# One PSUM bank with four kinds of users: features one stage later, transposes at other stages

## Chip, cores and metric

The kernel runs on one core of a Trainium2 chip. The metric is the device time of one execution in microseconds (us), as the median of several runs.

## What is computed

Input x has 32 images of 256 channels and 32 x 32 pixels. Two layers follow each other, each added to its own input:

```python
# layer 0: group norm, then a 3x3 convolution as a product of values rounded to 16-bit floats
x = x + conv3x3(quantize(group_norm(x)), quantize(weight)) + bias
# layer 1: group norm, then an involution: a 7x7 kernel for each pixel, made from the pixel's features
n = group_norm(x)                                # 32 groups of 8 channels
y = relu(batch_norm(w1 @ n))                     # 256 -> 64 features
w = w2 @ y + b2                                  # 16 groups x 49 taps for each pixel
x = x + sum over the 49 taps of w[group, tap, pixel] * shifted n[channel, pixel]
```

## The kernel before

**Work of an image.** The function `front` is a generator that does everything of an image up to its features: sums of both channel halves, means, squares, variances (class `GroupNorm`), the convolution in four units of 18 matmuls (two channel halves x 9 taps), the second group norm, the normalized image `xn`, then the features and the transposes. It gives way with `yield`, and what stands between two yields is a *stage*. The features are 64 matmuls into `py` (line 366), which ACT turns into `y_sb` (line 373). The transposes are four times: 16 matmul instructions on TensorE (PE) into `pt` (line 381) and one copy by ScalarE (ACT) into a buffer of `pixels` (line 385). Each `pixels` buffer holds one of the four stripes of 8 rows of the image; there are six.

**Involution.** `weights` multiplies the features of four rows by `w2` into PSUM (line 396), and VectorE (DVE) adds the bias and writes into the ring `w_sb` (line 414). `scatter` writes a stripe's weights with seven DMAs from the SP queue to `wd` in DRAM, in the order of a banded matrix (line 463). `load_bands` reads a *band* for the stripe back with 16 DMAs from the queue of GpSimd (POOL, line 475), into one of three buffers. `sums` multiplies the band by the pixels into PSUM (line 500), twice for each band (left and right side), and `add_windows` adds the result to x (line 516). `store` writes half an image.

**The order of work.** No planner sets it: a loop over steps n calls the parts, and each engine executes its instructions in that order. An image has 16 steps; several images are under way at once, each in another phase. The front of image b starts 58 steps ahead of its sums, and each step advances every open front by one stage, the oldest first. `yield LATER` puts the rest of a stage behind the stages of the other fronts in the same step. So stage s of any front falls in step (s + 6) mod 16, counted from the first sums of an image. In the same step, behind the fronts, come: sums in even steps (one side of one band, a new band in steps 0, 4, 8, 12), `add_windows` in odd ones, weights in even ones, a scatter in steps 3, 7, 11, 13 (bands 0 to 3 of a later image), a band's load in steps 3, 7, 11, 15, nine steps ahead of its use. The convolution's matmuls fall in odd steps, nine in each.

**The PSUM bank m.** The pool `ps_m` has a single buffer with the tag "m". Its users follow each other: the group sums `pg` of means (stages 3 and 29) and of variances (stages 6 and 31), each read by ACT at lines 228, 238 and 240; the features `py` (stage 38); the transposes `pt` (stages 44, 46, 48, 50). The matmuls of one user can't begin before ACT has read the user before.

Of the kernel before, what the change touches and what calls it, by code (L numbers as in the profile page):

```python
# [42 lines left out]
M = K * SIDES  # L43
# [26 lines left out]
def tile_quant_conv_then_involution(  # L70
# [201 lines left out]
    def front(b):  # L272


        xt = x_tiles[b]

        def stages(n):
            for _ in range(n):
                yield

        gn = GroupNorm()
        gn.begin(1)
        for h in range(CH):
            gn.add_up(xt, 0, h, 0, N, AF.Identity)
            yield
        yield
        yield LATER
        gn.means()
        gn.squares(xt)
        yield from stages(3)  # L290
        yield LATER
        gn.variances()
        yield
        gn.scales()
        yield
        gn.finish()

        for h in range(CH):
            yield
            gn.apply(h, [(xq[:, h], xt[:, h].rearrange("p (r c) -> p r c", c=W))])  # L300
        gn = GroupNorm()
        gn.begin(N // NT)
        units = [(nt, mh) for nt in range(N // NT) for mh in range(CH)]
        for s in range(4 * len(units) + 3):
            u, i = divmod(s, 4)
            if u < len(units):
                nt, mh = units[u]
                if i == 1:
                    pc = ps_c.tile([P, NT], F32, tag="pc", name="pc")
                for n in range(sum(CONV[:i]), sum(CONV[: i + 1])):  # L310


                    k = n if n < K0 * K0 else CH * K0 * K0 - 1 - n
                    kh, k = n // (K0 * K0), (k + K0 * K0 // 2) % (K0 * K0)
                    di, dj = k // K0 - PAD0, k % K0 - PAD0
                    r0, r1 = max(nt * RT, -di), min((nt + 1) * RT, H - di)
                    c0, c1 = max(0, -dj), min(W, W - dj)
                    nc.tensor.matmul(  # L318
                        pc.rearrange("p (r c) -> p r c", c=W)[:, r0 - nt * RT : r1 - nt * RT, c0:c1],
                        wq[:, kh, k, mh * P : (mh + 1) * P],  # L320
                        xq[:, kh, r0 + di : r1 + di, c0 + dj : c1 + dj],
                        start=n == 0,
                        stop=n == CH * K0 * K0 - 1,
                    )

            u, i = divmod(s - 4, 4)
            if 0 <= u < len(units) and i < 3:
                nt, mh = units[u]
                cols = slice(nt * NT, (nt + 1) * NT)
                if i == 0:  # L330
                    q = work.tile([P, NT], F16, tag="q", name="q", bufs=1)
                    nc.vector.tensor_scalar(q, pc, F16_MAX, -F16_MAX, ALU.min, ALU.max)  # L332
                elif i == 1:
                    nc.vector.scalar_tensor_tensor(  # L334
                        xt[:, mh, cols], q, bias_sb[:, mh : mh + 1], xt[:, mh, cols], ALU.add, ALU.add
                    )
                else:
                    gn.add_up(xt, nt, mh, nt * NT, (nt + 1) * NT, AF.Identity)
            yield
        yield LATER  # L340
        gn.means()
        gn.squares(xt)
        yield from stages(2)
        yield LATER
        gn.variances()
        yield
        gn.scales()
        yield from stages(2)
        gn.finish()
        xn = work.tile([P, CH, N], F32, tag="xn", name=f"xn_{b}", bufs=1)  # L350

        for h in range(CH):
            yield
            to = xn[:, h].rearrange("p (k d r j) -> p d k r j", d=SIDES, r=TR, j=JC)
            at = xt[:, h].rearrange("p (k r d j) -> p d k r j", d=SIDES, r=TR, j=JC)
            gn.apply(h, [(to[:, d], at[:, d]) for d in range(SIDES)])
        yield from stages(2)

        py = ps_m.tile([P, NT], F32, tag="m", name="py")
        for r0 in range(0, H, WR):  # L360
            cols = slice(r0 // 2 * W, (r0 + WR) // 2 * W)
            for kh in range(CH):
                px = xn[:, kh].rearrange("p (k d r j) -> p k r d j", d=SIDES, r=TR, j=JC)[:, r0 // TR]
                for i in range(2):
                    r = r0 % TR + 2 * i
                    nc.tensor.matmul(  # L366
                        py[i * CR : (i + 1) * CR, cols],
                        w1_sb[:, kh, :],
                        px[:, r : r + 2],
                        start=kh == 0,  # L370
                        stop=kh == CH - 1,
                    )
        nc.scalar.activation(y_sb[b % 2], py, AF.Relu, bias=bn_shift, scale=bn_scale)  # L373
        yield from stages(5)

        for m in range(0, M, 2):
            yield
            pt = ps_m.tile([P, 2, C], F32, tag="m", name="pt")
            for i in range(2):
                for h in range(CH):  # L380
                    nc.tensor.transpose(  # L381
                        pt[:, i, h * P : (h + 1) * P], xn[:, h, (m + i) * P : (m + i + 1) * P], ident
                    )
            to = pixels[(b * M + m) // 2 % NPIX].rearrange("p i a (v c) -> p (i a) v c", c=GC)
            nc.scalar.copy(to[:, :, ::2], pt.rearrange("p i (a v c) -> p (i a) v c", v=2, c=GC))  # L385
            yield

    def weights(b, r0):

# [142 lines left out]
    with tc.manual_schedule():  # L532
        fronts = {}
        for n in range(FRONT, B * per + 2):
            b, i = due(n, FRONT)
            if i == 0:
                fronts[b] = front(b)
# [74 lines left out]
```

## Time and profile before

| what | value |
| --- | --- |
| median of 4 runs (lowest to highest) | 1531.83 us (1525.14 to 1535.18) |
| the profiled execution | 1535.49 us, its span 1533.7 us |
| PE busy | 1317.9 us (86%), mean granted clock 0.958 |
| POOL busy | 1141.7 us (74%) |
| DVE, ACT busy | 865.5 us (56%), 741.8 us (48%) |
| mean busy share of the 16 DMA engines, 100 to 1400 us | 0.90, 252 GB/s |

A line of the page for a group of instructions reads: line of the kernel, engine, operation, what it writes <- what it reads, number; then busy time in us, mean ns of one, the engine's idle time ahead of them and what ended most of that. A line of the list of waits reads: engine and work that waited <- what ended the wait: us in total, times, longest. A line of a timeline reads: start in us, duration, engine, line, operation, number of instructions merged, and in brackets the idle time ahead of it with what ended it.

### The profile page before, as it was taken

How to read it: one execution, taken by the hardware profiler on the slowest of the kernel's cores; microseconds unless marked ns; L12 is line 12 of the kernel's file. 1: busy time of each engine (PE TensorE's matmuls, PEld its weight loads, DVE VectorE, ACT ScalarE, POOL GpSimd, SP SyncE). 2: the span in 40 equal slices, each digit the busy share in tenths (PEclk: the TensorE clock that was granted, in tenths of full speed). 3: DMA queues.
4: the chain of work that ended last, by engine and by line, in shares of the span. 5: the costliest groups of instructions: out<-in, count | busy, mean ns of one | idle time of the engine just before them, and what ended most of it. 6: DMA issues, size and time to landing. Idle time of an engine off the chain costs nothing.

```text
span 1533.7 us, 70106 instructions
## 1 busy us (share of the span) xinstructions
PE 1317.9 (86%) x29760; PEld 869.0 (57%) x29760; DVE 865.5 (56%) x2764; ACT 741.8 (48%) x1699; POOL 1141.7 (74%) x2068
## 2 busy tenths in 40 slices
PE   5899989889889988898988898898889899998764
PEld 2456656556556655565655565565556566665543
DVE  4356656655555655665556466565556565666452
ACT  5665555544554543555444455454446455553200
POOL 6068777768777787877777776877777777888786
PEclk9899999999999999999999999999999999999786
DMA  5089989898998898899899888898998799988885
GB/s 196 3 230 262 262 249 261 259 255 227 264 256 242 257 272 254 242 259 256 241 242 265 242 251 240 238 269 249 261 251 235 223 269 266 272 249 243 249 230 148
DMA packets 372375, 369.36 MB, mean 241 GB/s; under 512 B 84768, under 2 KB 314336, under 8 KB 371808
## 3 DMA queue, kind: packets, MB, share of 16 engines
q1 hardware_dynamic: 273760, 217.29, 48.4%
q0 software_dynamic: 98304, 147.59, 35.7%
q8 instruction: 236, 3.87, 1.1%
q14 instruction: 75, 0.61, 0.1%
HBM read 183.81 MB, written 180.74 MB: 238 GB/s over the span
## 4 chain that ended last, share of the span: by engine, by line
DMA 40%; PE 31%; POOL 14%; issue 6%; DVE 4%; ACT 3%; SPq 2%; POOLq 0%; ACTq 0%; DVEq 0%
DMA band<-wd 34%; POOL band L475 14%; PE pc L318 11%; PE acc L500 10%; PE pw L396 6%; DMA wd<-w_sb 5%; DVE w_sb L414 2%; SPq L463 2%; PE pt L381 2%; PE py L366 1%; PE pg L221 1%; ACT junk L213 1%; DVE x L516 1%; DVE w_sb L154 0%; ACT y L373 0%
## 5 line engine op out<-in xcount | busy, mean ns | idle before, releaser
L475 POOL DMA_DIRECT2D band<-wd x2048 | 1117.1, 548 | 377.6 <-DMA band<-wd 221.4
L414 DVE TENSOR_TENSOR w_sb<-pw,b_sb 128x16 f32<-128x16 f32 (+9 forms) x1920 | 454.0, 349 | 585.1 <-PE pw L396 584.0
L318 PE MATMUL pc<-xq,wq 128*128 128x496 f16 (+3 forms) x2304 | 541.4, 381 | 11.8 <-ACT xq L266 5.8
L500 PE MATMUL acc<-band,pixels 64*32 64x190 f32 (+1 forms) x16384 | 428.1, 331 | 130.7 <-DMA band<-wd 114.8
L500 PEld LDWEIGHTS acc<-band,pixels 64*32 64x32 f32 x16384 | 310.2, 110 | 205.4 <-issue 127.4
L318 PEld LDWEIGHTS <-wq 128*128 128x128 f16 x2304 | 208.1, 99 | 312.5 <-issue 110.2
L396 PE MATMUL pw<-w_sb,y 64*32 64x224 f32 (+1 forms) x8192 | 293.7, 341 | 1.3 <-issue 0.9
L516 DVE TENSOR_TENSOR x<-acc,x 128x380 f32<-128x380 f32 (+1 forms) x512 | 263.5, 515 | 39.1 <-PE acc L500 30.3
L213 ACT ACTIVATE junk<-x 128x512 f16<-128x512 f32 (+1 forms) x192 | 148.0, 771 | 141.7 <-DVE r L244 123.9
L396 PEld LDWEIGHTS pw<-w_sb,y 64*32 64x32 f32 x8192 | 189.0, 109 | 23.0 <-issue 8.5
L385 ACT COPY pixels<-pt 128x512 f32<-128x512 f32 x128 | 74.3, 580 | 258.4 <-PE pt L381 258.4
L213 ACT ACTIVATE junk<-x,mean 128x1024 f16<-128x1024 f32 x128 | 147.1, 1149 | 4.1
L332 DVE TENSOR_SCALAR q<-pc 128x512 f16<-128x512 f32 x128 | 87.2, 681 | 25.8 <-PE pc L318 25.8
L381 PE MATMUL pt<-ident,xn 128*128 128x128 f32 x512 | 80.6, 280 | 23.8 <-ACT ve L240 15.7
L266 ACT ACTIVATE xn<-x,off,rstd 128x512 f32<-128x512 f32 x128 | 96.1, 799 | 0.0
L334 DVE SCALAR_TENSOR_TENSOR x<-q,bias_sb,x 128x512 f32<-128x512 f16 x128 | 92.0, 718 | 0.4
L221 PEld LDWEIGHTS pg<-sums,avg 128*128 128x128 f32 x320 | 53.8, 193 | 56.5 <-ACT y L373 30.6
L266 ACT ACTIVATE xq<-x,off,rstd 128x1024 f16<-128x1024 f32 x64 | 78.7, 1233 | 9.6 <-PE pc L318 8.9
L228 ACT ACTIVATE mean<-pg 128x2 f32<-128x2 f32 x64 | 11.0, 171 | 148.6 <-PE pg L221 148.6
L381 PEld LDWEIGHTS pt<-ident,xn 128*128 128x128 f32 x512 | 58.6, 141 | 42.5 <-ACT ve L240 18.3
L221 PE MATMUL pg<-sums,avg 128*128 128x2 f32 x320 | 47.6, 232 | 37.6 <-ACT y L373 22.8
L366 PEld LDWEIGHTS py<-xn,w_sb 128*64 128x64 f32 x2048 | 64.4, 141 | 19.6 <-issue 9.3
(39 smaller groups left out, 375.4 us busy)
## 6 DMA issues: line engine op xcount, KB each, us to landing
band<-wd POOLq DMA_DIRECT2D x2048, 70.2 KB, 4.7
wd<-w_sb SPq DMA_DIRECT2D x896, 160.0 KB, 5.4
x<-in_x SPq DMA_DIRECT2D x64, 512.0 KB, 5.9
out<-x SPq DMA_DIRECT2D x64, 512.0 KB, 6.5
band<-in_w SPq DMA_DIRECT2D x2, 1152.0 KB, 8.4
w_sb<-in_w SPq DMA_DIRECT2D x2, 196.0 KB, 10.2
wd<-band SPq DMA_DIRECT2D x2, 180.0 KB, 3.8
b_sb<-in_b SPq DMA_DIRECT2D x7, 14.0 KB, 8.3
```

Source lines behind the costliest of these rows:

```text
L213: nc.scalar.activation(junk[:, n0:n1], src[:, h, n0:n1], func, bias=bias, accum_out=self.sums[:, part, h : h + 1])
L221: nc.tensor.matmul(pg[:, :CH], avg, self.sums[:, i, :], start=i == 0, stop=i == self.parts - 1)
L266: nc.scalar.activation(dst, src, AF.Identity, bias=self.off[:, one], scale=self.rstd[:, one])
L318: nc.tensor.matmul(pc.rearrange("p (r c) -> p r c", c=W)[:, r0 - nt * RT : r1 - nt * RT, c0:c1], wq[:, kh, k, mh * P : (mh + 1) * P], xq[: ...
L332: nc.vector.tensor_scalar(q, pc, F16_MAX, -F16_MAX, ALU.min, ALU.max)
L334: nc.vector.scalar_tensor_tensor(xt[:, mh, cols], q, bias_sb[:, mh : mh + 1], xt[:, mh, cols], ALU.add, ALU.add)
L381: nc.tensor.transpose(pt[:, i, h * P : (h + 1) * P], xn[:, h, (m + i) * P : (m + i + 1) * P], ident)
L396: nc.tensor.matmul(pws[i][t * TW : (t + 1) * TW, r, : dj.stop - dj.start], y_sb[b % 2][half, (r0 // 2 + r) * W : (r0 // 2 + r + 1) * W], w ...
L414: nc.vector.tensor_tensor(to, pws[i][:p, r : r + rows, e, d0 * G : d1 * G].rearrange("p r (d g) -> p r d g", g=G), b2_sb[:p, e, d0 * G : d ...
L475: nc.gpsimd.dma_start(band[j::JC, :, j * WB : j * WB + WPIX], src)
L500: nc.tensor.matmul(at[t * TW : (t + 1) * TW, h, :, f - top : l - top], px[p, a, v * GC : v * GC + TW], of[:, :, 2 * a + v, f - top : l - top],
L516: nc.vector.tensor_tensor(x_at, of, x_at, ALU.add)
```

## The change

The features come one stage later (39 instead of 38). The transposes, with their copies, come in stages 41, 44, 46 and 49 instead of 44, 46, 48 and 50. Nothing else is edited, and no buffer is added.

```diff
             gn.apply(h, [(to[:, d], at[:, d]) for d in range(SIDES)])
-        yield from stages(2)
+        yield from stages(3)
 
         py = ps_m.tile([P, NT], F32, tag="m", name="py")
...
         nc.scalar.activation(y_sb[b % 2], py, AF.Relu, bias=bn_shift, scale=bn_scale)
-        yield from stages(5)
-
-        for m in range(0, M, 2):
-            yield
+
+
+        for m, wait in zip(range(0, M, 2), (2, 3, 2, 3)):
+            yield from stages(wait)
             pt = ps_m.tile([P, 2, C], F32, tag="m", name="pt")
...
             nc.scalar.copy(to[:, :, ::2], pt.rearrange("p i (a v c) -> p (i a) v c", v=2, c=GC))
-            yield
```

## The prediction

> **What bounds the kernel now.** I read the busy lines of the page first, then the list of who waited for whom, then the timelines of POOL and PE over one image.
>
> ```profile
> PE 1317.9 (86%) x29760; PEld 869.0 (57%) x29760; DVE 865.5 (56%) x2764; ACT 741.8 (48%) x1699; POOL 1141.7 (74%) x2068
> ...
> L475 POOL DMA_DIRECT2D band<-wd x2048 | 1117.1, 548 | 377.6 <-DMA band<-wd 221.4
> ```
>
> By busy share PE looks like the bound. The second line says otherwise: POOL issues the 2048 band loads, 16 for each of 128 bands, at 548 ns each. Its first issue is at 83.7 us and its last ends at 1521.2, so 1437 us are there for 1117 us of issuing. The waits say what fills the other 320:
>
> ```profile
> POOL band L475 <- DMA band<-wd: 221.4, 252, 3.5
> PE acc L500 <- DMA band<-wd: 114.8, 54, 5.5
> POOL band L475 <- DMA wd<-w_sb: 71.7, 21, 57.1
> POOL band L475 <- issue: 53.8, 74, 3.8
> ...
> PE pg L221 <- ACT y L373: 22.8, 26, 0.9
> ...
> PE pt L381 <- ACT ve L240: 15.7, 31, 0.5
> ...
> PE pt L381 <- ACT mean L228: 8.1, 31, 0.3
> ...
> PE pg L221 <- DMA band<-wd: 3.5, 4, 0.9
> ```
>
> POOL waits mostly for its own earlier loads: the 16 issues of a band cycle through eight semaphores, and each needs the load eight places before it to have landed. Eight issues are 8 x 548 = 4.4 us, and the page gives 4.7 us from issue to landing as the median, so the landing decides. PE in turn waits 114.8 us for bands. The other four PE lines are the waits at the one PSUM bank m.
>
> ```profile
> 758.65 2.08 PE L318 MATMUL pc<-xq,wq 128*128 128x496 f16 x9
> 760.66 2.08 PE L366 MATMUL py<-xn,w_sb 128*64 128x64 f32 x64
> 763.62 0.38 PE L221 MATMUL pg<-sums,avg 128*128 128x2 f32 x2 [0.88 <-ACT y L373]
> 764.05 1.49 PE L500 MATMUL acc<-band,pixels 64*32 64x190 f32 x64
> ...
> 776.25 1.51 PE L500 MATMUL acc<-band,pixels 64*32 64x133 f32 x56 [3.58 <-DMA band<-wd]
> ```
>
> Here the features py, the wait for y, the variances pg, the sums. The bank costs PE 0.88 us, and 12 us later PE stands 3.58 us for a band. POOL in the same stretch:
>
> ```profile
> 759.78 8.17 POOL L475 DMA_DIRECT2D band<-wd  x15 [0.26 <-issue]
> 772.32 0.55 POOL L475 DMA_DIRECT2D band<-wd  x1 [4.37 <-DMA out<-x]
> 773.10 6.02 POOL L475 DMA_DIRECT2D band<-wd  x11 [0.23 <-DMA wd<-w_sb]
> ```
>
> It goes from one band into the next without a pause that PE sets. Over all bands, followed in the trace from image 3 to 28, a load begins about 10 us after its buffer was freed and 9 to 14 us after its scatter landed, and PE starts on it 0.5 to 2.5 us after its landing. So the loads are a closed loop of POOL and the DMA engines (busy share 0.90, 252 GB/s between 100 and 1400 us), and PE follows it: an image takes 45.3 us from band to band, of which PE needs 41.0.
>
> **What the Trainium skill says.** PSUM — Partial Sum Buffer, "PSUM bank collisions raise a hardware error", has a bank guarded by semaphores against two engines at once; the trace agrees in that pg starts only once ACT has read py (0.88 us). Perfetto Trace Analysis, "Optimization Strategy", takes a gap that repeats on the engine that should be saturated as a sign of too few buffers; here the gap repeats (31 times 0.5 us), but on an engine that is not the saturated one. Its "What 'DMA-bound' means" counts an issuing sequencer full of DMA slices as a bound of its own; POOL with 1117 us of issues and 275 of waits for its own queue fits. TensorE: Matmul & The Clock Gate, "What's actually happening", says that an idle window of about 3.4 us halves PE's clock: after the wait of 3.58 us above, the granted clock from 776 to 780 us was 0.62, so this case agrees.
>
> **The change, part by part.** Stage s of an image falls in step (s + 6) mod 16. Conv is issued in odd steps (2.08 us), sums (1.5 us) and weights (1.0 us) in even ones.
>
> Moved are, per image, the 64 matmuls of py with ACT's y, and four times 16 matmuls of a transpose with ACT's copy; none of them issues a DMA.
>
> *Variances behind y.* Both users were in step 12. py moves to 13, so pg no longer waits: 26 x 0.88 = 22.8 us, and 3.5 more that the list puts down to a DMA but that have the same 0.9 us. pg then is read by ACT (0.26 + 0.16 us) behind sums and weights, 2.5 us of PE work, before py wants the bank.
>
> *Transposes.* Stages 44, 46, 48, 50 (steps 2, 4, 6, 8) become 41, 44, 46, 49 (steps 15, 2, 4, 7). The one in step 6, right behind the variances of step 5, goes to 7: 15.7 us. The one in step 4 stays right behind the means of step 3: its 8.1 us remain. The one in 15 has conv, sums and weights (4.6 us) between it and y (0.78 us); the one in 7 has sums and weights between it and the variances. No new bank wait: 0, at most 0.3 us x 31 = 9.
>
> *y later.* The first weights of an image now stand one stage behind y instead of two. Between are conv and sums, 3.6 us against 0.78 of y: 0. Without a conv (last image) the sums still cover it. On ACT, y (0.78) and copies (0.58) change places with statistics of other images that wait on DVE anyway (123.9 us for r): 0.
>
> *Buffers.* pixels of band 3 are copied one step after their old readers, but the copy follows transposes that stand behind those readers on PE: 0. xn is free two stages ahead of its next writer, not one: 0. DVE, POOL and SP keep their order of instructions; only moments shift.
>
> Sum on PE: 22.8 + 3.5 + 15.7 = 42.0 us of waits gone, 1.35 an image. What is late next is the band: I cost this gain at nothing, because POOL's loop covers it; if that cover were gone it would be worth up to 42.
>
> *What reaches POOL.* The waits list has POOL released by PE for 7.2 + 6.7 + 2.5 + 0.2 = 16.6 us. I followed one (1.58 us at 1352, put down to pw): the band had been free for 12 us, and a landing of POOL's own queue came at that moment. I take a quarter, -4 us; bounds -16.6 and 0.
>
> *What the scatters do.* PE work between the first sums of successive bands is 10.5, 10.2, 11.9, 8.4 us for bands 0 to 3; after, 10.5, 10.2 - 0.66 - 0.51 = 9.0, 11.9 - 2.08 - 0.88 = 8.9, 8.4 + 2.08 + 0.66 = 11.2. So weights of step 12, and the scatter behind them, come up to 2.5 us earlier (band 3 was used 2.5 us after landing). The scatters of bands 2 and 3, 7.6 us apart, close up to some 5 us, about what SP takes to issue seven (5.2 us). Counting SP's DMAs in flight at each POOL issue, the next issue comes after 0.69 us with 2 to 5 in flight, 0.76 with 6, 0.88 with 7, 1.23 with 8, and 0.57 with none. For 2.5 us an image at 0.76 instead of 0.69, POOL loses 2.5 x (1/0.69 - 1/0.76) = 0.33 issues and gets as many back in the longer quiet that follows: 0. At 0.95 it loses 1.0, net 0.65 issues or 0.45 us, x 31 = 14. I take +2; bounds 0 and 14.
>
> Before the first load (83.7 us) one transpose comes ahead (0.66 us) and one wait goes (0.88): 0. The tail after the last front is untouched.
>
> Together -4 + 2 = -2 us on the profiled execution's 1535.5 (span 1533.7 and 1.8 around it). That execution was 3.7 above the median, so on the median of 1531.8 I say **1530 us**.
>
> **Rivals.** *PE was the path after all.* The chain that ended last has 31% on PE and 3% on ACT, and PE has 86% busy time, which speaks for it; the 10 us between a freed buffer and its load speak against. With the chain's share, 0.34 x 42 = 14 us: 1517; with all of it, 1490.
>
> *The close scatters slow POOL* (the other side). Place: the seven SP transfers of band 3 on top of those of band 2, with the 0.5 MB store between. Price: 14 us, 1546. It decides once SP has 7 or 8 in flight for over some 1.3 us more in each image (half the price, 7 us). Against it: SP's own issue time keeps the two apart by 5.2 us.
>
> *The change does not part the users.* One pair stays (step 4), 8.1 us; if the rest stayed as well, the time would be 1532.
>
> **How the numbers follow.** Covered by POOL's loop, or nothing parted: 0.54, with 1524 to 1538 as its own range. PE on the path: 0.28. Scatters too close: 0.18. A measurement of this kernel can tell about 0.5% from no change, 7.7 us: below 1524.2 is faster, above 1539.5 slower. The covered case leaks 0.01 upward, so faster 0.28, same 0.53, slower 0.19. The range goes from 1506 (most of the first rival) to 1546 (the second's price), leaving out the full 42 us and worse mishaps, somewhat under 2 in 10.
>
> **What would show it.** Right: pg waits for y near 0, pt for ve near 0, pt for mean still about 8; acc waits for bands grow by some 30 to 45 us from 114.8; POOL's last issue stays near 1521 us, its own-queue waits near 275. Wrong: acc waits for bands stay near 115 while the span shrinks (PE was the path), or POOL's own-queue waits grow by over 8 us together with scatters 2 and 3 closer than 6 us. The forecast as a whole is wrong if POOL's time from first to last issue changes by more than 8 us.

## The result: 0.26% slower, and the profile after

The changed kernel takes 1538.14 us in the median of 44 runs, the kernel before 1532.39 us in that of 63. The ratio is 1.0026, with a 95% interval of 1.0011 to 1.0041; it leaves disturbed runs out, which the medians don't. That is 4.0 us (1.7 to 6.3) of loss where a gain of 2 was forecast. The range held the time, the direction was wrong.

The list of waits of the changed kernel (line numbers behind line 386 are lower by one: L474 is the band load, L499 the sums, L395 the weights):

```profile
POOL band L474 <- DMA band<-wd: 234.0, 264, 2.8
PE acc L499 <- DMA band<-wd: 129.2, 71, 5.3
POOL band L474 <- DMA wd<-w_sb: 75.4, 31, 54.4
POOL band L474 <- issue: 51.6, 79, 2.8
...
PE py L366 <- issue: 18.9, 11, 3.5
...
PE acc L499 <- issue: 15.8, 17, 1.6
...
PE pw L395 <- issue: 9.5, 7, 3.4
...
PE pt L381 <- ACT mean L228: 8.1, 31, 0.3
```

The bank's waits went as planned: pg no longer waits for y, pt no longer for ve, and the one pair in step 4 kept its 8.1 us. So 42 us of PE's waits are gone. The list also says what took their place: 14.4 us more for bands (129.2 instead of 114.8), and 32 us more of "issue", idle time that no semaphore ended (47.9 us over all its PE rows; 15.8 before). Both sums come from one execution of each kernel, and the sum of "issue" swings: in kernels below that keep the bank's waits it is 33 to 55 us. PE's timeline shows one of these stops:

```profile
403.76 1.49 PE L499 MATMUL acc<-band,pixels 64*32 64x190 f32 x64 [1.20 <-DMA band<-wd]
404.95 1.06 PE L395 MATMUL pw<-w_sb,y 64*32 64x224 f32 x32
405.93 0.44 PE L366 MATMUL py<-xn,w_sb 128*64 128x64 f32 x6
408.93 2.40 PE L366 MATMUL py<-xn,w_sb 128*64 128x64 f32 x58 [2.56 <-issue]
```

PE stops after 6 of the 64 matmuls of py, where no semaphore is waited for. In the DMA records of the trace, a packet of 16 KB on the instruction queue ends at 407.58 us, 1.35 us ahead of the seventh. The 30 such stops of over 0.6 us beyond 150 us all end 1.2 to 1.7 us behind the end of such a packet, and so do all six before. So PE most likely waits for its own instructions here.

What sets the end is POOL's queue. Its row for the band loads in the view of the band tile, of the kernel before and of the changed one (last numbers: start of the first issue to start of the last):

```profile
L475 POOL DMA_DIRECT2D band<-wd x2048: 547/547/683, 83.7 to 1520.7; - x187
```

```profile
L474 POOL DMA_DIRECT2D band<-wd x2048: 547/547/681, 81.0 to 1524.0; - x187
```

The first load starts 2.7 us earlier, and the last 3.3 us later: the same 2048 issues take 1443.0 us instead of 1437.0. In both kernels the span ends 13 to 14 us after the start of the last issue, and in all kernels below that issue the 2048 loads from POOL it is 12.7 to 14.1. The 6 us themselves are the difference of two executions: over the single profiles below this time goes from 1434.5 to 1455.8 us, and not in the order of the timed ratios.

Part of the earlier start goes with PE's clock. The row of the windows view for 54 to 68 us (length, busy of PE, PEld, DVE, ACT, POOL, then PE's granted clock, DMA share, GB/s), before and after:

```profile
54.00:68.00 14.00, 9.50 (x109) 5.82 (x108) 1.46 (x4) 9.28 (x22) 0.00 (x0) 0.63 0.00 1
```

```profile
54.00:68.00 14.00, 10.66 (x152) 7.16 (x152) 2.71 (x11) 9.52 (x24) 0.00 (x0) 0.76 0.01 2
```

The records of the clock have it halved for 10.2 us before (from 56.8 to 67.0) and for 6.8 us after (55.3 to 62.1). At half speed 3.4 us are worth up to 1.7 us of PE's time, an estimate. PE's waits in this stretch are about as long in all (4.7 and 4.5 us) but otherwise divided, the longest 3.62 and 2.77 us; that this is what moves the clock was not tested. And 0.75 us of the 2.7 is there already at 42 us, ahead of the features, so about 2.0 us belong to the change. All ten kernels with the features in stage 39 show 0.76 or 0.88 here, and a first load at 80.0 to 81.5 us; the others, but for the one with py twice (0.76), show 0.63 and 81.9 to 83.8.

### The profile page after: what moved, and what is told of

The parts are those of the page before. It is cut to its first block, busy times and chain, and to the rows that moved or that the text cites. A ratio compares the mean times of both kernels' runs of the same rounds, so it can differ in the third digit from the quotient of the medians.

```text
span 1538.0 us, 70165 instructions
## 1 busy us (share of the span) xinstructions
PE 1314.2 (85%) x29760; PEld 870.6 (57%) x29760; DVE 868.9 (56%) x2764; ACT 734.2 (48%) x1699; POOL 1141.8 (74%) x2068
## 4 chain that ended last, share of the span: by engine, by line
DMA 37%; PE 36%; POOL 13%; issue 6%; DVE 4%; SPq 3%; ACT 1%; POOLq 0%; DVEq 0%; ACTq 0%
DMA band<-wd 30%; PE pc L318 14%; POOL band L474 13%; PE acc L499 11%; PE pw L395 7%; DMA wd<-w_sb 6%; SPq L462 3%; DVE w_sb L413 2%; PE py L366 2%; PE pt L381 2%; PE pg L221 1%; ACT junk L213 1%; DVE x L515 0%; DVE w_sb L154 0%; DMA out<-x 0%
## 5 line engine op out<-in xcount | busy, mean ns | idle before, releaser
L474 POOL DMA_DIRECT2D band<-wd x2048 | 1117.2, 548 | 380.8 <-DMA band<-wd 234.0
L499 PE MATMUL acc<-band,pixels 64*32 64x190 f32 (+1 forms) x16384 | 423.9, 328 | 146.7 <-DMA band<-wd 129.2
L499 PEld LDWEIGHTS acc<-band,pixels 64*32 64x32 f32 x16384 | 305.5, 109 | 223.8 <-issue 133.0
L318 PEld LDWEIGHTS <-wq 128*128 128x128 f16 x2304 | 213.7, 99 | 293.1 <-issue 90.8
L395 PE MATMUL pw<-w_sb,y 64*32 64x224 f32 (+1 forms) x8192 | 296.5, 340 | 10.9 <-issue 9.5
L395 PEld LDWEIGHTS pw<-w_sb,y 64*32 64x32 f32 x8192 | 187.9, 109 | 35.3 <-issue 18.3
L373 ACT ACTIVATE y<-py,bn_shift,bn_scale 128x512 f32<-128x512 f32 x32 | 24.9, 777 | 181.5 <-PE py L366 181.5
L366 PE MATMUL py<-xn,w_sb 128*64 128x64 f32 x2048 | 73.3, 230 | 21.7 <-issue 18.9
```

The costliest lines, as they stand in the source:

```text
L318: nc.tensor.matmul(pc.rearrange("p (r c) -> p r c", c=W)[:, r0 - nt * RT : r1 - nt * RT, c0:c1], wq[:, kh, k, mh * P : (mh + 1) * P], xq[: ...
L366: nc.tensor.matmul(py[i * CR : (i + 1) * CR, cols], w1_sb[:, kh, :], px[:, r : r + 2], start=kh == 0, stop=kh == CH - 1,)
L395: nc.tensor.matmul(pws[i][t * TW : (t + 1) * TW, r, : dj.stop - dj.start], y_sb[b % 2][half, (r0 // 2 + r) * W : (r0 // 2 + r + 1) * W], w ...
L474: nc.gpsimd.dma_start(band[j::JC, :, j * WB : j * WB + WPIX], src)
L499: nc.tensor.matmul(at[t * TW : (t + 1) * TW, h, :, f - top : l - top], px[p, a, v * GC : v * GC + TW], of[:, :, 2 * a + v, f - top : l - top],
```

## Experiments

All ratios are to the kernel before, run beside on the same chip. Distances of scatters are medians over the images of one profile, from start to start. A single profile is one execution out of a spread of more than 1%, so small differences are read from the timed ratios, not from profiles.

### The change, its halves, and the features twice

The changed kernel again, for a measure on the same chip:

> The changed kernel once more, as the measure for the other three. Whatever the theory: 1.001 to 1.004 of the kernel before. Theory A (POOL's loop of band loads sets the time, and its own-queue waits grew): POOL's waits for its own loads again some 5 to 10 us above the 275 us of before. Theory B (PE is the path, and the 42 us that it no longer waits for ACT came back as waits for instructions): PE idle time without a releaser near 48 us again, against 16 before.

Measured: 1.0035 (1.0009 to 1.0060). POOL's waits for its own loads are 296.5 us, 21 above before instead of 5 to 10; PE's waits without a releaser 61.8.

Only the features later (of the changed kernel):

```diff
-        for m, wait in zip(range(0, M, 2), (2, 3, 2, 3)):
+        for m, wait in zip(range(0, M, 2), (5, 2, 2, 2)):
```

> Features in stage 39, transposes where they were (44, 46, 48, 50). Takes away the wait of pg for y (26 us) and keeps the wait of pt for ve (15.7 us). Theory A, with the scatters of bands 2 and 3 brought closer by py leaving the gap between them: the whole loss is here, ratio 1.002 to 1.004. Theory B: PE loses waits for ACT and takes on waits for instructions in py, since sums, weights and py (320 instructions) now follow each other without a conv between: idle time of py without a releaser some 15 to 20 us, ratio 1.001 to 1.003. Theory C (a moved transpose does it): ratio 0.999 to 1.001.

Measured: 1.0045 (1.0020 to 1.0070). The scatters of bands 2 and 3 start 6.85 us apart; PE's py waits 16.8 us without a releaser. The whole loss is here, as Theory A had it. But the 16.8 us is what Theory B expected; the late weights below part the two.

Only the transposes moved (of the changed kernel):

```diff
-        yield from stages(3)
+        yield from stages(2)
...
-        for m, wait in zip(range(0, M, 2), (2, 3, 2, 3)):
+        for m, wait in zip(range(0, M, 2), (3, 3, 2, 3)):
```

> Features in stage 38 as before, transposes in 41, 44, 46, 49. Keeps the wait of pg for y and takes away that of pt for ve (15.7 us). Theory A: neither the gap of scatters 2 and 3 nor POOL's queue changes, ratio 0.999 to 1.001. Theory B: no new wait for instructions, 15.7 us off a path on PE, ratio 0.99 to 0.998. Theory C: ratio 1.002 to 1.004.

Measured: 1.0015 (0.9985 to 1.0044), not to be told from no change. The distance of the scatters stays at 7.4 us. Theory B's gain is excluded, Theory C's loss not quite. Waits without a releaser rose to 50.8 us here too, none of them at py: they don't all come from py standing behind weights, as Theory B has it.

The features twice:

```diff
-        for r0 in range(0, H, WR):
+        for r0 in [*range(0, H, WR)] * 2:
```

> The kernel before, with the 64 matmuls of the features issued twice (the second pass starts the sums anew, so the values are the same): 2.08 us more PE work in each image, 66 us over all, and one more stretch of dense instructions. Theory A: PE has 4.3 us of waits in an image to take it from, so the time rises by at most 8 us (ratio below 1.005) and the waits of acc for bands fall from 115 to some 50 us. Theory B: the time rises by most of 66 us, ratio 1.03 to 1.04.

Measured: 1.0016 (0.9989 to 1.0042). From its page and its list of waits:

```profile
PE 1372.4 (89%) x31808; PEld 918.3 (60%) x31808; DVE 865.9 (56%) x2764; ACT 741.8 (48%) x1699; POOL 1141.8 (74%) x2068
```

```profile
PE acc L500 <- DMA band<-wd: 45.8, 22, 5.2
```

PE has 54.5 us more busy time than before (1372.4 against 1317.9), its wait for bands falls by 69 us, and the time moves by at most 0.42%, 6.4 us. The last scatter also comes later here (9.3 us behind that of band 2 instead of 7.4), and late weights by themselves, below, gave a ratio of 0.9973. So some 4 us of cost may be hidden, an estimate, still little beside 54.5. PE's work is thus covered for the most part, and so was what the bank cost it. This decides against the first rival of the prediction.

### The distance of two scatters

The last weights of the changed kernel a step later, behind py and conv:

```diff
-            if b is not None and i % 2 == 0:
-                weights(b, i // 2 * WR)
+            if b is not None and (i % 2 == 0 and i < 2 * M - 2 or i == 2 * M - 1):
+                weights(b, (i + 1 if i == 2 * M - 3 else i) // 2 * WR)
```

> The changed kernel, with the last weights of an image (four rows, step 12) a step later, behind py and conv, so that the scatter of band 3 follows that of band 2 by about 10 us instead of 6.9 and SP has a pause between them. Theory A (the scatters of bands 2 and 3, back to back on SP, slow POOL's loads): the loss goes, ratio to the kernel before 0.997 to 1.001, POOL from first to last issue back to 1436 to 1442 us. Theory B (waits for instructions in PE): ratio stays 1.002 to 1.005.

Measured: 0.9992 (0.9963 to 1.0021), with 8.8 us between the scatters. PE's waits without a releaser are 52.2 us here, no less than the 47.9 with the loss: in these profiles they don't go with the time, as Theory B would have it.

The last weights of the kernel before a step earlier (the same edit with `i == 2 * M - 3` in the place of `i == 2 * M - 1` in the condition; the rows stay the same):

> The kernel before, with the last weights of an image a step earlier, ahead of py, so that the scatter of band 3 is ready some 5 us earlier and SP issues scatters 2 and 3 without a pause, at some 6.5 us instead of 7.4. The features and transposes stay in their stages, and pg still waits for y. Theory A: the loss of the change without the change, ratio 1.002 to 1.005, POOL's gaps up by 6 us or more. Theory B: ratio 0.999 to 1.001.

Measured: 1.0028 (1.0003 to 1.0053), with 6.7 us. The features are where they were and pg waits for y as ever, and the loss is there. The expected rise of POOL's gaps doesn't show in its single profile (317.9 us, 320.5 before), but that execution took 1531.8 us where the median of this kernel is 1544.0.

SP's timelines show what the two distances mean. The columns are start, length, then the DMAs issued; first before, then the changed kernel, then that with late weights:

```profile
739.10 26.35 SPq L463 DMA_DIRECT2D wd<-w_sb  x21
765.55 0.78 SPq L521 DMA_DIRECT2D out<-x  x1
767.62 6.37 SPq L463 DMA_DIRECT2D wd<-w_sb  x7
```

```profile
773.29 1.06 SPq L520 DMA_DIRECT2D out<-x  x1
774.71 7.08 SPq L462 DMA_DIRECT2D wd<-w_sb  x7
781.89 0.73 SPq L520 DMA_DIRECT2D out<-x  x1
```

```profile
766.54 1.12 SPq L520 DMA_DIRECT2D out<-x  x1
770.29 4.97 SPq L462 DMA_DIRECT2D wd<-w_sb  x7
775.36 0.98 SPq L520 DMA_DIRECT2D out<-x  x1
```

Between the store's issue and the scatter of band 3 SP pauses 1.3 us before (767.62 - 765.55 - 0.78), 0.4 after, 2.6 with late weights. In the changed kernel SP thus issues 7 scatters, a store, 7 scatters and a store almost without a pause, and the seven of band 3 take 7.1 us, against 6.4 before and 5.0 with late weights (one image each; the medians over the images are 7.0, 6.8 and 5.4).

Late weights in the kernel before (the same edit):

> The kernel before, with the last weights of an image in step 13 instead of 12, as in the changed kernel with late weights (0.999). Theory A1 (what counts is the pause on SP between the scatters of bands 2 and 3: 6.9 us between their starts costs, 8.8 does not): 7.4 becomes some 8.5 to 9.5 us, ratio 0.996 to 0.9995. Theory A2 (the old 7.4 us are as good as any, only falling below the 6.9 us at which SP has no pause costs): 0.999 to 1.001.

Measured: 0.9973 (0.9939 to 1.0007), with 9.6 us. It lies at Theory A1's place, but the interval just reaches no change. If late weights help the kernel before as well, they may cancel a loss of any cause: with late weights in both, the change stands at 0.9992 / 0.9973 = 1.0019, with some 0.45% either way, too wide to tell. What speaks for the cause by itself is the kernel before with early weights, whose interval lies just clear of no change.

Features a stage later and late weights:

> The features a stage later, transposes where they were (1.0045 by itself), with the last weights in step 13. Theories A1 and A2: the loss goes, 0.997 to 1.001. Theory E (py in step 13 costs by its place, not by the scatters): 1.002 to 1.006.

Measured: 0.9981 (0.9960 to 1.0002), with 9.0 us, against 1.0045 (1.0020 to 1.0070) for the same kernel without late weights. The intervals don't meet, and Theory E's range is missed: py may stand in step 13, provided that the weights don't come earlier for it. A small cost of its place isn't excluded, since late weights may gain something by themselves. PE's waits without a releaser are 44.2 us, against 34.1 with the loss: again they don't go with the time.

The store behind both scatters:

```diff
-            b, i = due(n, 2)
+            b, i = due(n, 4)
             if b is not None and i == 2 * (M - 1 - SIDES):
                 store(b, 0)
```

> The changed kernel with the store of the first half image two steps later, behind the scatter of band 3 instead of between those of bands 2 and 3. SP then issues the two scatters directly after each other, some 5.5 to 6 us between their starts instead of 6.9. Theory A1 and A2: more loss, 1.004 to 1.010. Theory F (the store between them, three transfers of different kinds in a row, is what costs): less, 0.998 to 1.002. Theory E: 1.002 to 1.004, as the changed kernel.

Measured: 1.0040 (1.0018 to 1.0062), with 5.9 us. SP's timeline has the 28 scatter DMAs of an image's four bands merged, and the two stores behind them:

```profile
745.82 34.54 SPq L462 DMA_DIRECT2D wd<-w_sb  x28
780.41 1.83 SPq L520 DMA_DIRECT2D out<-x  x2
```

So the store between the scatters was not what cost (Theory F). Whether 5.9 us is worse than 6.9 can't be told from this.

Four scatters spread over the image, in the changed kernel and in the one before:

```diff
-            if b is not None and i % 2 == 0:
+            if b is not None and i % 2 == 0 and i < 2 * M - 2:
                 weights(b, i // 2 * WR)
+            b, i = due(n, -LEAD + 3)
+            if b is not None and i == 2 * M - 2:
+                weights(b, i // 2 * WR)
+                scatter(b, K - 1)
...
-                for k in range(K):
+                for k in range(K - 1):
```

> The changed kernel, with the last weights of an image and the scatter of band 3 in step 15 instead of 12 and 13, so that the four scatters of an image lie some 10 to 12 us apart (now 10.3, 10.1, 6.9, 16.1). Theory A (two scatters back to back slow POOL's loads): a stronger dose of the late weights, ratio to the kernel before 0.993 to 0.999. If the spacing is no cause (Theory E: the loss comes with the place of py and not with the scatters): ratio 1.001 to 1.005.

> The same spacing in the kernel before, whose scatters lie 10.8, 9.7, 7.4 and 16.0 us apart. Theory A: also faster than the kernel before, ratio 0.993 to 0.999, and about level with the changed kernel so spaced (within 0.3%). Theory E: ratio 0.999 to 1.001.

Measured: 1.0045 (1.0015 to 1.0075) and 1.0080 (1.0042 to 1.0117). Both misses. Scatters 2 and 3 are now 13.8 us apart, but 3 and the next 0 only 8.0 to 8.2, with a store's landing and the two loads of x (512 KB each) between them. The expectation had counted scatters alone. By the place of their issues the burst was not taken apart but moved to another spot, where x is loaded; that this is why it costs more is argued, not shown.

The prediction had named a sign for scatters that come too close: SP with 7 or 8 DMAs in flight for over some 1.3 us more in each image. Counted from issue to landing in the traces, over 28 images, it is 2.6 us an image before and 2.9 and 2.7 in two profiles of the changed kernel; such a mean is good to about 0.4 us. It is 2.9 with early weights, but 3.2 to 3.5 in the three kernels with late weights, which lose nothing; 4.1 with the store behind the scatters; 5.6 and 5.5 with the even spacing. So the number in flight fits the loss of the even spacing and perhaps of the late store. It does not explain that of the change. In all five kernels that lose with scatters of bands 2 and 3 at 5.9 to 6.9 us, the last weights stand ahead of py; what this does to POOL's loads stays open.

### POOL's loop out of the way

```diff
-            nc.gpsimd.dma_start(band[j::JC, :, j * WB : j * WB + WPIX], src)
+            queue = nc.sync if i % 4 == 3 else nc.gpsimd
+            queue.dma_start(band[j::JC, :, j * WB : j * WB + WPIX], src)
```

> The kernel before, with 4 of the 16 loads of each band issued from SP instead of POOL. POOL's loop of a band then has 12 issues of 0.68 us, 8.2 us instead of 11. Theory A (POOL's loop sets the time): the time falls until PE or the DMA engines set it: 41 us of PE work and 1.7 us of waits at bank m in an image, so some 1.43 ms, ratio 0.94 to 0.98, and PE's waits for bands nearly vanish. Theory D (the DMA engines as a whole, at a busy share of 0.90, set it, whoever issues): ratio 0.99 to 1.01. Theory B: 0.99 to 1.01 too.

> The changed kernel with the same relief. Theory A: with POOL's loop out of the way the waits at bank m lie on the path, and this one is faster than the relieved kernel before by some 20 to 42 us (1.3 to 2.7%), less what waits for instructions take back. Theory D: it stands to the relieved kernel before as the changed one to the kernel before, slower by 0 to 0.5%.

Measured: 0.9633 (0.9592 to 0.9674) and 0.9593 (0.9551 to 0.9634); medians 1479.6 and 1474.0 us. The relief is what Theory A expected, and Theory D (whoever issues, the DMA engines set the time) is out. The difference of 5.6 us between the two is far less than the 20 to 42 expected, and the intervals overlap.

The same with the even spacing on top:

> The changed kernel with 4 of 16 band loads on SP (0.959 of the kernel before) and the even spacing on top. With PE at 90% and the DMA engines at a busy share near 0.97 in that kernel, Theory A leaves little for the spacing: ratio to the kernel before 0.950 to 0.962.

> The kernel before with 4 of 16 band loads on SP and the even spacing, to set beside the changed kernel with both (0.9405 of the kernel before, 1448 us). In that regime PE is busy for 90% of the span, so the 42 us of waits at bank m should be worth most here. If they reach the end: 0.950 to 0.965, the changed one being better by 1 to 2.5%. If waits for instructions and the DMA engines take them back: 0.940 to 0.948.

Measured: 0.9405 (0.9366 to 0.9443), 1448.2 us, and 0.9615 (0.9579 to 0.9651), 1478.7 us. Here the change is worth 0.9405 / 0.9615 = 0.978, 2.2%, and the intervals are well apart. From 100 to 1400 us (columns as above), before and after:

```profile
100.00:1400.00 1300.00, 1199.69 (x27663) 778.26 (x27664) 797.45 (x2558) 673.64 (x1543) 778.42 (x1427) 0.99 0.94 259
```

```profile
100.00:1400.00 1300.00, 1216.90 (x28386) 794.21 (x28376) 811.82 (x2627) 667.06 (x1545) 803.02 (x1472) 0.99 0.96 267
```

In the same 1300 us PE gets through 28386 instead of 27663 matmuls, 2.6% more, and the DMA engines move 267 GB/s instead of 259. The gain of 30.5 us fits the 38.5 us of waits at the bank that the list has for the one before (22.8 + 15.7) and no longer for the changed one, so most of them seem to reach the end here, although PE's waits without a releaser are 58 us in the changed one and 49 in the other. The changed kernel with relief and even spacing is the fastest of all. Why the spacing helps the relieved changed kernel (1474.0 to 1448.2 us) and not the relieved one before (1479.6 to 1478.7) was not tried.

### Instructions in a row

The features summed over half the channels, in the changed kernel:

```diff
-            for kh in range(CH):
+            for kh in range(1):
...
-                        start=kh == 0,
-                        stop=kh == CH - 1,
+                        start=True,
+                        stop=True,
```

> The changed kernel with the features summed over the first 128 of the 256 channels only (the other half of the 64 matmuls of py is left out, so the values are not the reference's). Sums, weights and py are then 256 instead of 320 instructions in a row, in 3.5 us. If PE's waits without a releaser (49 to 62 us in two profiles of the changed kernel, 16 before) come from instructions that are fetched too slowly for this stretch, those at and behind py nearly vanish and their sum falls to 10 to 30 us. If they have another cause: 45 to 65 us again. The time stays within 1% of the changed kernel in both cases.

Measured (one execution): 1547.2 us, PE's waits without a releaser 53 us. A miss for the sum. At py itself they are 9.3 us, against 18.9 and 24.0 in the two profiles of the changed kernel, but the other lines have more (43.7 against 29.0 and 37.8). That the stops end just behind the landing of an instruction packet stands; which stretches cause them stays open.

## Why the prediction was wrong

**What bounds the kernel: right.** POOL's loop sets the end. The features twice (at most 0.42% for 54.5 us of PE busy time) and the relief (3.7% for a quarter of the loads) show it. The prediction sees in POOL a queue full of issues; but the issues fill 1117 of 1437 us, and waits for landings most of the rest (221.4 us), so how soon the loads land counts as well. A transpose is 4 matmul instructions, 16 in an image, and not 16 four times as the texts above have it; the 0.66 us of the sums was measured, so nothing hangs on it.

**The bank's waits: right in size, and rightly costed at nothing.** The 42 us went, the 8.1 us stayed.

**What is late next: half right.** The band took 14 us of the 42, not the 30 to 45 named as the sign. The other 32 went, in this pair of profiles, into stops that look like waits for instructions, which the prediction did not have. Kernels that keep the bank's waits have such stops too (34.3 us in the one before with late weights), so the change is not shown to cause them. Runtime: NRT & Kernel Launch, "Instruction fetch mechanics", has the sequencer refill its buffer in blocks of 16 KiB, 256 instructions, by a DMA queue of its own, and takes that as mostly hidden. This trace agrees on the block (236 packets of 16 KB on that queue). It agrees on "mostly" by count, since only 6 stops of over 0.6 us follow such packets before and 30 after, but these and the smaller ones still cost 16 and 48 us of PE's time, at a DMA busy share of 0.90.

**What reaches POOL, -4 us: failed.** The waits put down to PE fell from 16.6 to 10.6 us, but POOL's first-to-last time grew. The one that had been followed ended with a landing of POOL's own queue, which spoke for 0; the others were not followed, then or later.

**What the scatters do, +2 us: the step that decided, mis-sized.** The direction was there: work leaves the stretch between the weights of steps 10 and 12, and the scatters of bands 2 and 3 close up. Two terms were wrong. The distance was put at 5 us and is 6.9, since the store's issue stands between. And the price was netted to nearly nothing, as though the quiet afterwards paid it back. The loss that was measured, 4.0 us beside a start that is 2.0 to 2.7 us earlier, makes it some 6 to 7 us by estimate, 0.2 us for each image. That lies in the middle of the bounds of 0 to 14.

The mechanism is only half confirmed. Of the signs named for it, POOL's waits for its own queue grew by 10.4 us (over 8 was named), but the scatters are not closer than 6 us, POOL's time from first to last issue grew by 6.0 and not by 8, and SP has 7 or 8 in flight for 0.3 us more in an image, not 1.3. The experiments tie the loss to the early weights: five kernels that have them lose 0.26 to 0.45%, and three with late weights lose nothing that can be told. That close scatters are the link was not isolated, since moved weights shift DVE's writes too, and the count of DMAs in flight speaks against the form of it that was priced.

**Ahead of the first load, 0: failed,** -2.7 us, some 2.0 of it from the change, and most of that fits PE's clock. The prediction had quoted the clock's rule but not asked what the change does to it at the start.

## What to carry to other kernels

A wait that goes from an engine which follows another one's queue bought nothing here, but it moved everything that this engine triggers; ask first which queue those transfers share with the bound, and at what distance they now follow each other. Test the bound by giving the suspected engine more work: 54.5 us more on PE for no more time than could be measured told more than any list of waits. And keep such a change for the day the bound is gone: with a quarter of the loads off POOL and the scatters spread, the same edit was worth 2.2%.

## What the runs showed of the hardware

- POOL's loads, with eight semaphores to cycle through, come slower with more of the other queue's traffic: in the kernel before the next issue came after 0.57 us with no SP transfer in flight, 0.69 us with 2 to 5 (0.74 with one), and 0.88 us with 7.
- PE stands without a releaser until 1.2 to 1.7 us after a packet of 16 KB on the instruction queue ended: single stops of up to 3.7 us, 48 and 62 us in all in two profiles of the changed kernel, 16 in the one before.
- One stage's difference in order changed PE's granted clock between 54 and 68 us from 0.63 to 0.76.
